# The DMAs of two output blocks, issued behind the next stage's first subtraction on GpSimd

## The chip, the cores and the metric

The kernel runs on one core of one Trainium2 chip. The metric is the device time of one launch in microseconds (us), the median of several runs. Beside it stands the profile of one execution. Its names for the engines are PE (TensorE, matmul), PEld (TensorE's weight load), DVE (VectorE), ACT (ScalarE), POOL (GpSimd) and SP (SyncE, which issues DMAs here); SPq and POOLq are the instruction queues of the last two. "L934" is line 934 of the kernel.

## The reference

Eight images of 512 channels, 32 x 32 pixels, float32. Each is group-normalized, goes through a C2f block with two attention bottlenecks, and is added to the input:

```python
x = x + _L0_conv_ref(_gn(x), ...)          # out = x + block(group_norm(x))

t = cbs(x, cv1_w, cv1_bn, 0)               # 1x1 conv 512 -> 512, batch norm, SiLU
ys = [t[:, :C], t[:, C:]]                  # C = 256
for i in range(N):                         # N = 2 bottlenecks
    yi = ys[-1]
    z = cbs(yi, m_cv1_w[i], m_cv1_bn[i], 1)                  # 3x3 conv 256 -> 256
    z = bot_attention(z, m_qkv_w[i], m_rw[i], m_rh[i])       # 4 heads of 64 over 1024 positions
    z = silu(bn_eval(conv2d(z, m_cv2_w[i], 0), m_cv2_bn[i])) # 1x1 conv
    ys.append(yi + z)
return cbs(concatenate(ys, axis=1), cv2_w, cv2_bn, 0)        # cv2: 1x1 conv 1024 -> 512
```

## The kernel before

**Pairs of images.** A loop `for p in range(NP)` treats the images in four pairs: the first image `ia` (a) and the second `ib` (b). In each pair, for bottleneck n = 0 and then n = 1, one 3x3 convolution (`conv3x3`) serves both images, and then the attention runs for image a and for image b. Work of other stages is put between the attention's steps: the group norm of the next pair, its cv1, and the final cv2. The convolution of n = 0 is called in this text the first one of the pair, that of n = 1 the second one.

**cv2 by blocks.** cv2 is one matrix product per image, 512 x 1024 times 1024 x 1024. `strassen` computes it as a 2 x 2 block product with seven block products. The result has four blocks, which `finish(i, ...)` puts out: i = 0 is C11, 1 is C12, 2 is C22, 3 is C21. `finish` works on two channel parts (`at` = 0, 1): ScalarE applies the SiLU into a tile `c_out`; a DMA from GpSimd's queue adds the input `x` from DRAM to that tile (`accum_op=ALU.add`, L1500); a second one stores the tile to `out` (L1501). The store must wait until the accumulating DMA has landed. That wait stands in GpSimd's own instruction queue, so everything queued behind it on GpSimd waits too.

For the second image of the pairs p = 0, 1, 2, `strassen` gets an argument `l2`: three of its seven products are then computed by quarter blocks (`by_quarters3`). In this variant `finish` gets a tile name (`room`) for two blocks: C12 with `l2.spare[0]`, the tile `p1`, and C21 with `l2.spare[1]`, the tile `p2`. C11 and C22 use a ring of four smaller tiles, `t`, and have no `room`. The last pair (p = 3) doesn't use `strassen` but other functions, with `finish` functions of their own. Image a of p = 0, 1, 2 goes through `strassen` without `l2`.

**Where the end of a pair meets the next one.** `part3` returns the last step, `lambda: finish(3, u3, l2.spare[1])`, which the loop keeps as `last_out`. The next pair hands it to its first convolution as `after`; it runs there behind the first PSUM copy on ScalarE. So C21 of one pair is put out while the next pair's first convolution is under way; C12 is put out just before it.

**The convolution and the projections behind it.** `conv3x3` runs over two output channel halves (`oc`) and three row groups (`i`), with products on PE, a PSUM copy on ScalarE (L680), and combinations on VectorE. The SiLUs of channel half 0 come when that half is done. In the second half, at `oc = 1, i = 1`, `conv3x3` calls `first_sum(summed, nc.gpsimd)`, which makes `t_z`, the difference of the two halves of the positions of channel half 0 of `z` (L934). The queries, keys and values are then computed by `project_strassen`, also a 2 x 2 block product. Its first products read `z`, the next ones read `t_z`:

```python
to_qk(ps_a, w["11"], b11)
if early:
    early()
to_qk(ps_b, w["s1"], t1)
```

(`t1` is `t_z`.) `project_strassen` also loads the position terms, `r_in` (L982), which VectorE adds at L986. The attention's first products are `l_ps` (L1080). In pair 0 the first convolution is another variant: it calls no `first_sum`.

**What sets the order.** Each engine runs its instructions in the order of its queue. A scheduler makes that order from the order in the program text; `tc.issue_after(ins)` adds that the instructions in its block come behind `ins` on the engine of `ins`. Around the change, GpSimd's queue holds the DMAs of `finish`, small memsets, the subtraction L934, and later the power and product of the group norm (L780, L837). SP's queue holds the loads: weights (`u`, `sq`, `sw`), the next images (`x`), `r_in`.

Of the kernel before, what the change touches and what calls it, by code (L numbers as in the profile page):

```python
# [48 lines left out]
ALU = mybir.AluOpType  # L49
# [13 lines left out]
def kernel(  # L63
# [16 lines left out]
    nc = tc.nc  # L80
# [8 lines left out]
    HALF = 512  # L89
# [107 lines left out]
    for tag in "qk":  # L197
        t = act.tile([P, NX // 2, HW], F32, tag=tag, name="x_second")
# [163 lines left out]
    def take_blocks(kind, n, which, names):  # L362
# [9 lines left out]
        out=gmat, in_=gmat, compare_op=ALU.is_ge, fill=0.0, base=0,  # L372
# [3 lines left out]
        out=gmat, in_=gmat, compare_op=ALU.is_ge, fill=0.0, base=GROUP - 1,  # L376
# [9 lines left out]
    spare = const.tile([P, 1], F32, name="spare")  # L386
# [111 lines left out]
    def by_slot(ap):  # L498
        a = ap.rearrange("p (h w) -> p h w", w=F) if len(ap.shape) == 2 else ap
        return a.rearrange("p h (j s) -> p h j s", j=4)  # L500

    def from_planes(ap):

        a = ap.rearrange("p (h w) -> p h w", w=F) if len(ap.shape) == 2 else ap
        return bass.AP(tensor=a.tensor, offset=a[:, :, 3:].offset, ap=[a.ap[0], a.ap[1], [-1, 4], [4, NT]])
# [7 lines left out]
    def stages(act, small, ps_big, ps_av, n_pt):  # L513

        def silu(dst, src, k):

            silued[0] = nc.scalar.activation(  # L517
                dst, src, AF.Silu, scale=sh[:, k : k + 1], bias=bh[:, k : k + 1]
            )
            return silued[0]  # L520
# [111 lines left out]
        def conv3x3(n, vs, u_of, z, groups=G, summed=None, after=None, between={}, silus=None):  # L632
# [10 lines left out]
            for oc in range(NM):  # L643
                dst = z[:, oc].rearrange("p g x -> p (g x)").rearrange("p (t r w) -> p r t w", r=4, w=F)
                for i in range(NI):
# [57 lines left out]
                    for (at, size), m in zip(parts, m_parts):  # L703
# [28 lines left out]
                        if i == 1:  # L732
                            if oc == NM - 1 and summed is not None:
                                t = first_sum(summed, nc.gpsimd)
# [154 lines left out]
        def project_direct(n, z, w, early=None, middle=None):  # L889
# [38 lines left out]
                qk(c)  # L928
            return q, kr, vT, lambda: None

        def first_sum(z, engine=nc.vector):

            t = act.tile([P, 2, HALF], F32, tag="pt", name="t_z", bufs=n_pt)
            engine.tensor_tensor(t[:, 0], z[:, 0, ts(1, HALF)], z[:, 0, ts(0, HALF)], ALU.subtract)  # L934
            return t

        def project_strassen(n, z, w, t, early=None, middle=None, table=False, silus=()):
# [517 lines left out]
        def strassen(b, ws, top, tags, tile_of, l2=None):  # L1455
# [34 lines left out]
            def rows_of(dram, i, at):  # L1490
                o, half = blocks[i]
                return dram[b, ts(2 * o + at, P), ts(half, HALF)]

            def finish(i, src, room=None):
                o, half = blocks[i]
                both = act.tile([P, 2, HALF], F32, tag=room, name="c_out") if room else None
                for at in range(2):
                    t = both[:, at] if room else act.tile([P, HALF], F32, tag="t", name="c_out", bufs=4)
                    silu(from_planes(t), by_slot(src[:, at, :]), bn_cv2 + 2 * o + at)
                    nc.gpsimd.dma_start(t, rows_of(x, i, at), accum_op=ALU.add)  # L1500
                    nc.gpsimd.dma_start(rows_of(out, i, at), t)  # L1501

            def part3(bottom, after=None):
                t1 = kept["t1"]
# [19 lines left out]
                for part in range(2):  # L1524
                    product(ps1, w12, bottom[0], [part], onto=True)
                    product(ps5, s4, bottom[1], [part], onto=True)
                finish(0, ps1)

                def new(name, t):
# [5 lines left out]
                c12 = tile_of("o1")  # L1535
                tt(c12, ps5, m1, ALU.add)
                finish(1, c12)
                tt(m1, new("s3", t3), m1, ALU.add)
                tt(m5, m5, m1, ALU.add)
                finish(2, m5)  # L1540
                tt(m1, m1, new("22", t4), ALU.subtract)
                return lambda: finish(3, m1)
# [404 lines left out]
    ps_big = fast.enter_context(tc.tile_pool(name="ps_big", bufs=3, space=PSUM))  # L1947
    ps_av = fast.enter_context(tc.tile_pool(name="ps_av", bufs=1, space=PSUM))
    s = stages(act, small, ps_big, ps_av, 6)

    def held(tag):
# [256 lines left out]
    for (i, cp), u in first_units.items():  # L2208
        fed["u", 0, 0, i, cp] = u

    last_out = None
    for p in range(NP):
        ia, ib = G * p, G * p + 1
        more = p + 1 < NP
# [3 lines left out]
        def u_of(n):  # L2218
            return lambda oc, i: [take(("u", n, oc, i, cp)) for cp in range(3)]

        def new_z():
            return act.tile([P, NM, G, HW], F32, tag="z", name="z")
# [50 lines left out]
        def direct_keys(which):  # L2273
# [6 lines left out]
        z = new_z()  # L2280
        silus = []
        t = s.conv3x3(
            0, vs, u_of(0), z, summed=None if direct else z[:, :, 0], after=last_out,
            between=in_first if direct else {}, silus=None if direct else silus,
        )
        xs = norm = None
        if more:
            if direct:
# [86 lines left out]
        if more and not direct:  # L2375
# [11 lines left out]
            with tc.issue_after(last.ins):  # L2387
                t = s.first_sum(z[:, :, 1])
# [7 lines left out]
        else:  # L2396
            if not direct:
                t = s.first_sum(z[:, :, 1])
# [139 lines left out]
        z = new_z()  # L2538
        t = s.conv3x3(1, vs, u_of(1), z, summed=z[:, :, 0], silus=silus)
# [80 lines left out]
        if not more:  # L2620
# [23 lines left out]
            l2 = SimpleNamespace(of=l_of, room=x_room)  # L2644
# [90 lines left out]
        def room_b(name):  # L2735
# [5 lines left out]

        b1, b1_more, b2, b3 = s.strassen(
            ib, w_of, top, {"m1": ("p3", 1), "m5": ("p4", 1)}, tile_of,
            SimpleNamespace(of=l_of, room=room_b, spare=("p1", "p2"))
        )
        b1()
        b1_more()
# [14 lines left out]
        last_out = b3(bottom)  # L2762
# [19 lines left out]
    with tc.If(held_all < P):  # L2782
        with ExitStack() as gs:
# [4 lines left out]
            make_identity(nc, ident)  # L2788
            g_av = gs.enter_context(tc.tile_pool(name="g_av", bufs=2, space=PSUM))
            g = stages(g_act, g_small, g_big, g_av, 3)  # L2790
            with tc.For_i(0, B, 1) as b:
                xts = [load_x(g_act, b, c, NX) for c in range(NX)]
# [6 lines left out]
                for n in range(N):  # L2799
# [5 lines left out]
                    z = g_act.tile([P, NM, 1, HW], F32, tag="z", name="z")  # L2805
# [69 lines left out]
```

## Time and profile before

| | us |
|---|---|
| median of three runs | 2239.03 (2238.82 to 2239.42) |
| the profiled execution | 2240.72 |
| its span, from the first to the last instruction | 2239.2 |
| DVE busy in the span | 1803.2 |
| ACT busy | 1093.4 |
| POOL busy | 223.3 |

The mean granted clock of TensorE is 0.993 of full speed. A group of instructions in the profile is one line, engine, operation and tile, with its count, its busy time, the mean of one in ns, the idle time of the engine just ahead of it, and what ended that idle time ("<-"). A timeline row has start, duration, engine, line, operation, output tile <- input tiles, shape and count; in brackets stands the idle time before it with its releaser. Matmuls are pipelined and their ends are modelled: distances between starts are safer than durations.

### The profile page before, as it was taken

What the parts mean: (1) busy time and instruction counts of PE and PEld (TensorE: products, weight loads), DVE (VectorE), ACT (ScalarE), POOL (GpSimd) and SP (SyncE); (2) the same over time, 40 slices, a digit from 0 to 9 for tenths busy, and PEclk for the clock granted to TensorE, in tenths of its full rate; (3) what the DMA queues carried; (4) which work ended last, traced back from release to release, by engine and by line L of the source; (5) the groups of instructions that cost most, each with busy time, mean ns of one, the idle gap of its engine ahead of it and who ended that gap; (6) DMA issues with size and microseconds to landing.
All of it is one profiled execution on the core that took longest, in us unless ns stands there. A gap on an engine that the chain in (4) does not pass through costs nothing.

```text
span 2239.2 us, 40840 instructions
## 1 busy us (share of the span) xinstructions
PE 2189.4 (98%) x16486; PEld 1112.7 (50%) x16486; DVE 1803.2 (81%) x2935; ACT 1093.4 (49%) x1320; POOL 223.3 (10%) x409
## 2 busy tenths in 40 slices
PE   7999999999989999999998999999999899999998
PEld 3653438343574444734457443564346734373445
DVE  8988879878887688977887768997787777897676
ACT  7455553654225666456323676455622365436543
POOL 4322210000220000000022000000002100000001
PEclk9999999999999999999999999999999999999999
DMA  8954447312591324512259141542126711251224
GB/s 269 314 163 141 160 148 257 100 48 71 155 310 48 115 84 135 194 59 67 69 138 306 33 153 47 179 140 77 58 67 180 274 39 40 95 192 39 76 58 114
DMA packets 135528, 291.93 MB, mean 130 GB/s; under 512 B 33732, under 2 KB 61376, under 8 KB 134308
## 3 DMA queue, kind: packets, MB, share of 16 engines
q1 hardware_dynamic: 102708, 201.01, 27.2%
q0 software_dynamic: 32624, 88.23, 13.3%
q8 instruction: 132, 2.16, 0.4%
q14 instruction: 64, 0.52, 0.1%
HBM read 219.58 MB, written 69.60 MB: 129 GB/s over the span
## 4 chain that ended last, share of the span: by engine, by line
PE 76%; DVE 8%; issue 7%; DMA 6%; POOL 1%; ACT 1%; SPq 0%; POOLq 0%; DVEq 0%; ACTq 0%
PE av_ps L1117 19%; PE l_ps L1080 18%; PE p_ps L956 7%; PE c_ps L675 6%; PE x_ps L1767 4%; PE m_ps L1334 4%; DMA c_out<-in_x_dram 4%; PE ps L545 4%; PE p_ps L962 3%; PE c L1354 3%; PE c_q L1402 2%; PE c_new L1354 2%; PE s_ps L1135 1%; DMA taps<-in_m_cv_w_dram 1%; PE c_new L1386 1%
## 5 line engine op out<-in xcount | busy, mean ns | idle before, releaser
L1084 ACT ACTIVATE pt<-l_ps 128x1024 f32<-128x1024 f32 x512 | 495.6, 1023 | 328.2 <-PE l_ps L1080 252.3
L1080 PE MATMUL l_ps<-q,kr 64*64 64x512 f32 x4096 | 485.5, 590 | 0.9 <-ACT pt L1084 0.9
L1117 PE MATMUL av_ps<-pt,vT 64*64 64x512 f32 x4096 | 484.7, 590 | 1.3 <-DVE z L1125 1.1
L1101 DVE TENSOR_TENSOR acc<-acc,pt 128x1024 f32<-128x1024 f32 x362 | 442.5, 1222 | 36.9 <-ACT pt L1084 9.8
L1117 PEld LDWEIGHTS av_ps<-pt,vT 64*64 64x64 f32 x4096 | 156.1, 133 | 280.6 <-issue 234.3
L1080 PEld LDWEIGHTS l_ps<-q,kr 64*64 64x64 f32 x4096 | 157.5, 133 | 270.3 <-issue 246.6
L675 PE MATMUL c_ps<-v_in,u 128*64 128x128 f32 x4320 | 238.5, 273 | 0.0
L675 PEld LDWEIGHTS c_ps<-v_in,u 128*64 128x64 f32 x4320 | 235.8, 137 | 4.9 <-issue 4.7
L956 PE MATMUL p_ps<-t_z,sq 128*128 128x512 f32 x224 | 111.6, 622 | 19.1 <-POOL t_z L934 19.1
L1125 DVE TENSOR_TENSOR z<-av_ps,z 128x512 f32<-128x512 f32 x64 | 43.9, 686 | 98.4 <-ACT z L1124 98.2
L1334 PE MATMUL m_ps<-z,m_sb 128*128 128x512 f32 x256 | 114.2, 593 | 0.1
L680 ACT COPY c_m<-c_ps 128x512 f32<-128x512 f32 x48 | 28.1, 585 | 152.4 <-PE c_ps L675 138.8
L517 ACT ACTIVATE t<-m_ps,bh,sh 128x512 f32<-128x512 f32 x64 | 46.3, 773 | 95.3 <-PE m_ps L1334 94.1
L1098 DVE TENSOR_TENSOR acc<-pt 128x1024 f32<-128x1024 f32 x64 | 78.0, 1219 | 14.2 <-PE s_ps L1135 8.7
L956 PE MATMUL p_ps<-z,sq 128*128 128x512 f32 x168 | 81.1, 603 | 0.7 <-ACT z L517 0.7
L1334 PEld LDWEIGHTS m_ps<-z,m_sb 128*128 128x128 f32 x256 | 47.7, 190 | 57.1 <-issue 51.4
L956 PEld LDWEIGHTS p_ps<-t_z,sq 128*128 128x128 f32 x224 | 40.7, 198 | 58.3 <-issue 34.7
L1193 DVE TENSOR_TENSOR z<-z,rs 128x512 f32<-128x512 f32 x64 | 42.3, 685 | 31.6 <-DMA rs<-r_dram 31.4
L517 ACT ACTIVATE z<-z,bh,sh 128x512 f32<-128x512 f32 x64 | 48.7, 809 | 25.2 <-DVE z L737 25.1
L962 PEld LDWEIGHTS p_ps<-sq,z 128*128 128x128 f32 x336 | 46.2, 201 | 23.8 <-issue 14.8
L1767 PE MATMUL x_ps<-t_x,sw 128*128 128x512 f32 x128 | 55.9, 592 | 0.0
L517 ACT ACTIVATE c_out<-c,bh,sh 128x512 f32<-128x512 f32 x12 | 14.0, 1277 | 85.7 <-PE c L1386 61.7
(408 smaller groups left out, 3301.7 us busy)
## 6 DMA issues: line engine op xcount, KB each, us to landing
u<-u SPq DMA_DIRECT2D x135, 512.0 KB
y_in<-y SPq DMA_DIRECT2D x32, 512.0 KB
rs<-r_dram SPq DMA_DIRECT2D x126, 128.0 KB
sq<-sq SPq DMA_DIRECT2D x42, 384.0 KB
x<-in_x_dram SPq DMA_DIRECT2D x28, 512.0 KB
r_in<-r SPq DMA_DIRECT2D x28, 512.0 KB
c_out<-in_x_dram POOLq DMA_DIRECT2D x56, 256.0 KB, 6.8
out_dram<-c_out POOLq DMA_DIRECT2D x56, 256.0 KB, 3.7
```

The source lines that it names most:

```text
L517: silued[0] = nc.scalar.activation(dst, src, AF.Silu, scale=sh[:, k : k + 1], bias=bh[:, k : k + 1])
L545: last_product[0] = nc.tensor.matmul(ps[:, half, :], w_of(k), rhs_of(k, half), start=(k == begin), stop=(k == end))
L675: conv_product[0] = nc.tensor.matmul(to[o], us[cp][:, k, row, c, o], rhs, start=(k == 0), stop=(k == NM - 1),)
L956: nc.tensor.matmul(ps[:, o, :], w[:, o, :], rhs, start=not onto, stop=True, skip_group_check=onto)
L962: nc.tensor.matmul(v[:, ts(j, P)], rhs[:, ts(j, P)], w[:, 2, :], start=j == 0 and not onto, stop=True, skip_group_check=True,)
L1080: nc.tensor.matmul(ps[kh * HD : (kh + 1) * HD, hd, :], kr[r, c, o : o + HD], q[r, c, ts(half, HALF)], start=True, stop=True,)
L1084: last_exp[0] = exp = nc.scalar.activation(pt, ps, AF.Exp, scale=SCALE)
L1101: ins = nc.vector.tensor_tensor(accs[g], accs[g], pt[i], ALU.add)
L1117: nc.tensor.matmul(avs[g][hd * HD : (hd + 1) * HD, kh, :], vT[r, j, o : o + HD], pt[i][r, hd, :], start=(j == 0), stop=(j == NJ - 1),)
L1334: nc.tensor.matmul(pss[half][:, oc, :], m2_sb[:, n, k, ts(oc, P)], ao[:, k, ts(half, HALF)], start=(k == 0), stop=(k == NM - 1),)
L1354: nc.tensor.matmul(ps[:, o, :], w[:, k, ts(o, P)], rhs[part][:, c], start=(k == 0 and not onto), stop=(k == KB - 1), skip_group_check=onto,)
L1767: nc.tensor.matmul(ps[:, o, :], w[:, c, ts(o, P)], rhs[c], start=(c == 0 and not onto), stop=(c == 1), skip_group_check=onto,)
```

## The change

`first_sum` keeps its instruction in `summing[0]`. In `finish`, the two DMAs of a channel part become a function `put_out`; where the block has a `room` (C12 and C21 of the second image), it isn't called but appended to the list `l2.late`. The next pair calls the functions in that list directly behind its first convolution's call, under `issue_after` with the kept subtraction. The SiLUs stay where they were, and so do the DMAs of C11 and C22.

```diff
+        summing = [None]
+
         def first_sum(z, engine=nc.vector):
 
             t = act.tile([P, 2, HALF], F32, tag="pt", name="t_z", bufs=n_pt)
-            engine.tensor_tensor(t[:, 0], z[:, 0, ts(1, HALF)], z[:, 0, ts(0, HALF)], ALU.subtract)
+            summing[0] = engine.tensor_tensor(t[:, 0], z[:, 0, ts(1, HALF)], z[:, 0, ts(0, HALF)], ALU.subtract)
             return t
...
                     silu(from_planes(t), by_slot(src[:, at, :]), bn_cv2 + 2 * o + at)
-                    nc.gpsimd.dma_start(t, rows_of(x, i, at), accum_op=ALU.add)
-                    nc.gpsimd.dma_start(rows_of(out, i, at), t)
+
+                    def put_out(t=t, at=at):
+                        nc.gpsimd.dma_start(t, rows_of(x, i, at), accum_op=ALU.add)
+                        nc.gpsimd.dma_start(rows_of(out, i, at), t)
+
+                    if room:
+                        l2.late.append(put_out)
+                    else:
+                        put_out()
...
-    last_out = None
+    last_out, late_outs = None, []
...
             0, vs, u_of(0), z, summed=None if direct else z[:, :, 0], after=last_out,
             between=in_first if direct else {}, silus=None if direct else silus,
         )
+        if late_outs:
+            with tc.issue_after(s.summing[0].ins):
+                while late_outs:
+                    late_outs.pop(0)()
...
-            SimpleNamespace(of=l_of, room=room_b, spare=("p1", "p2"))
+            SimpleNamespace(of=l_of, room=room_b, spare=("p1", "p2"), late=late_outs)
```

The list is filled in the pairs 0, 1 and 2 and emptied in the pairs 1, 2 and 3: each time four functions, eight DMAs.

## The prediction

> **What bounds the kernel now.** I read the page first (busy time, chain, costliest groups), then the chain of work between 625 and 700 us, then the timelines of GpSimd, ScalarE, VectorE and TensorE there. From the page:
>
> ```profile
> PE 2189.4 (98%) x16486; PEld 1112.7 (50%) x16486; DVE 1803.2 (81%) x2935; ACT 1093.4 (49%) x1320; POOL 223.3 (10%) x409
> ...
> L956 PE MATMUL p_ps<-t_z,sq 128*128 128x512 f32 x224 | 111.6, 622 | 19.1 <-POOL t_z L934 19.1
> ```
>
> TensorE (PE) is busy 98% of the span, so a change pays only where PE stands still or runs slowly. Of its idle time 19.1 us stands in one group: products on `t_z`, the tile that `first_sum` (line 934) writes on GpSimd. The GpSimd timeline shows why `t_z` is late:
>
> ```profile
> 646.52 1.82 POOL L1500 DMA_DIRECT2D c_out<-in_x_dram  x2
> 655.56 0.58 POOL L1501 DMA_DIRECT2D out_dram<-c_out  x1 [7.22 <-DMA c_out<-in_x_dram]
> ...
> 658.48 1.82 POOL L1500 DMA_DIRECT2D c_out<-in_x_dram  x2
> ...
> 670.50 0.57 POOL L1501 DMA_DIRECT2D out_dram<-c_out  x1 [2.29 <-DVE c_e L716]
> 671.08 1.27 POOL L934 TENSOR_TENSOR t_z<-z 128x512 f32<-128x512 f32 x1
> ```
>
> These are the blocks C12 and C21: two accumulating DMAs, two stores that wait for them to land, and the same again. GpSimd keeps its order, so the subtraction, last in the queue, starts at 671.08. Its input was long ready:
>
> ```profile
> 653.91 2.93 ACT L517 ACTIVATE z<-z,bh,sh 128x512 f32<-128x512 f32 x4 [1.79 <-DVE z L737]
> ```
>
> Those four SiLUs write the channel half that the subtraction reads; it needs the first two, done after about half of 2.93 us, near 655.4. What PE does meanwhile:
>
> ```profile
> 663.61 1.98 PE L956 MATMUL p_ps<-z,sq 128*128 128x512 f32 x4
> 672.41 3.78 PE L956 MATMUL p_ps<-t_z,sq 128*128 128x512 f32 x4 [6.82 <-POOL t_z L934]
> ...
> 677.60 1.06 PE L962 MATMUL p_ps<-sq,t_z 128*128 128x128 f32 x8
> ...
> 691.64 3.66 PE L1080 MATMUL l_ps<-q,kr 64*64 64x512 f32 x32
> ```
>
> The convolution ends at 663.61, four products on `z` follow, PE stands 6.82 us, and the first products afterwards take double.
>
> The kernel holds its own control: the second convolution of each pair ends in the same code (`conv3x3`, then `project_strassen`), with no stores ahead of the subtraction.
>
> ```profile
> 912.38 2.93 ACT L517 ACTIVATE z<-z,bh,sh 128x512 f32<-128x512 f32 x4 [3.16 <-DVE z L737]
> ...
> 913.98 1.27 POOL L934 TENSOR_TENSOR t_z<-z 128x512 f32<-128x512 f32 x1 [24.11 <-ACT z L517]
> ...
> 920.78 1.98 PE L956 MATMUL p_ps<-z,sq 128*128 128x512 f32 x4
> 922.60 1.88 PE L956 MATMUL p_ps<-t_z,sq 128*128 128x512 f32 x4
> ...
> 925.21 1.06 PE L962 MATMUL p_ps<-sq,t_z 128*128 128x128 f32 x8
> 926.43 1.98 PE L956 MATMUL p_ps<-z,sq 128*128 128x512 f32 x4 [0.17 <-ACT z L517]
> ...
> 939.96 3.66 PE L1080 MATMUL l_ps<-q,kr 64*64 64x512 f32 x32
> ```
>
> Here the subtraction starts 1.60 us after the SiLUs, and PE goes through at full pace. The table by stage, three first convolutions and then two of the second ones, each from the first `p_ps` product to attention:
>
> ```profile
> 663.60:691.70 28.10, 21.29 (x90) 0.88 0.52 171
> 1213.40:1240.90 27.50, 21.61 (x90) 0.88 0.55 179
> 1763.00:1790.70 27.70, 21.34 (x90) 0.88 0.56 184
> 920.70:940.00 19.30, 19.11 (x92) 1.00 0.48 156
> 1470.20:1489.50 19.30, 19.10 (x91) 1.00 0.49 158
> ```
>
> The columns are the window, its length, PE's busy time (instructions), granted clock, DMA share and GB/s. The same work takes 27.5 to 28.1 us with an 0.88 clock in one place and 19.3 us with a full clock in the other.
>
> **The change part by part.** *The move.* In each of the three pairs p = 1, 2, 3, eight GpSimd instructions (four accumulating DMAs, four stores) go from ahead of the subtraction to behind it. SiLUs, SP's DMAs and TensorE's order stay. The subtraction loses 671.08 − (653.91 + 1.60) = 15.6 us of queueing and would end near 656.8; PE wants it at 663.61 + 1.82 = 665.4 (1.82 is the step from 920.78 to 922.60). That leaves 8.6 us of cover, so the whole wait goes.
>
> *What it is worth.* I take the control's duration for all three places: 939.96 − 920.78 = 19.18 us. The places themselves, by their first and last rows:
>
> ```profile
> 1213.40 1.98 PE L956 MATMUL p_ps<-z,sq 128*128 128x512 f32 x4
> ...
> 1240.83 1.52 PE L1080 MATMUL l_ps<-q,kr 64*64 64x512 f32 x12
> ...
> 1763.03 1.98 PE L956 MATMUL p_ps<-z,sq 128*128 128x512 f32 x4
> ...
> 1790.66 1.93 PE L1080 MATMUL l_ps<-q,kr 64*64 64x512 f32 x13
> ```
>
> 691.64 − 663.61 = 28.03, 27.43 and 27.63: together 83.09, less 3 x 19.18 = 57.54, gives **25.5 us**. It splits into the 19.1 us of idleness and 6.4 us beside it. In the first place the products from 672.41 to 677.60 take 5.19 us, and the same ones in the control, from 922.60 to 925.21, 2.61: 2.6 us go to the slow clock, and some 0.5 of them the control loses in waits of its own (0.17 <-ACT z).
>
> *What is late next.* In the control, the next bounds are ScalarE's SiLU of the other channel half and VectorE's tail of the convolution. VectorE stands as follows relative to PE:
>
> ```profile
> 655.33 0.68 DVE L716 SCALAR_TENSOR_TENSOR c_e<-c_ps,c_t 128x512 f32<-128x512 f32 x1
> ...
> 913.79 0.68 DVE L716 SCALAR_TENSOR_TENSOR c_e<-c_ps,c_t 128x512 f32<-128x512 f32 x1
> 914.39 1.15 DVE L725 SCALAR_TENSOR_TENSOR c_r<-c_t 128x256 f32<-128x256 f32 x1
> 915.46 0.41 DVE L723 SCALAR_TENSOR_TENSOR c_r<-c_t,c_e 128x256 f32<-128x256 f32 x1
> ...
> 670.67 1.97 DVE L736 SCALAR_TENSOR_TENSOR z<-c_r,c_k 128x256 f32<-128x256 f32 x1
> ```
>
> It starts L716 8.28 us ahead of the first `p_ps` product (663.61 − 655.33), in the control 6.99 (920.78 − 913.79): it is 1.29 us better placed, so the control's waits shrink if anything. At best they go: the 0.19 us in which PE isn't busy in the control's window (19.30 − 19.11) and 0.10 for a group that restarts (1.98 at 926.43, 1.88 at 922.60), 0.9 us over three places: 26.4.
>
> *The collision with VectorE.* While the subtraction runs, a VectorE instruction is held: 1.97 us at 670.67, where a 128x256 one takes 0.41 (915.46). Moved, the subtraction hits VectorE inside its unbroken run; in the control that makes one instruction 1.15 instead of 0.41, 0.74 us, and this is already in the 19.18. The ends are nothing and 1.56 us each place, 4.7 in all, if the hold is as long as at 670.67 and comes out whole at PE; I take the control's, because its phase is the same (0.18 us after L716 begins, here 655.51 − 655.33).
>
> The Trainium skill (SBUF — State Buffer, SBUF: two separate sides) calls the port that these two engines share an exclusive lock, held for a whole instruction; that speaks against moving the subtraction into VectorE's busiest stretch. By it the hold could be the full 1.27 us, an estimate of 1.6 us more over three places than the control's; the trace shows a longer hold, 1.97 − 0.41 = 1.56 us, and the rows decide.
>
> *The moved DMAs.* Issues take 0.57 to 0.91 us each beside VectorE instructions of usual length (0.68 for 128x512 at 655.33), so issuing costs the other engines nothing visible. Behind them on GpSimd stands:
>
> ```profile
> 730.69 1.04 POOL L780 TENSOR_TENSOR gr<-gr,mhalf 128x4 f32<-128x4 f32 x1 [58.34 <-DVE gr L779]
> ...
> 1900.14 1.22 POOL L2368 DMA_DIRECT2D v<-v_new  x2 [128.82 <-DVE v_new L622]
> ```
>
> Two rounds of accumulate and store took 24.6 us (646.52 to 671.08). Begun at 656.8 they end near 681, and the next GpSimd instruction, some 9 us earlier than now, comes at 722: 41 us of cover, more in the last pair (1900). The tiles `p1` and `p2`, which now stay occupied until then, are next written by ScalarE behind the attention that follows (cv1's SiLUs, in the last pair the copies of m1 and m5). The transfers leave a stretch where the DMA engines are full and reach one where they have room:
>
> ```profile
> 658.40:671.00 12.60, 7.19 (x102) 5.71 (x98) 12.53 (x47) 1.60 (x2) 2.98 (x5) 0.99 1.05 368
> 671.00:691.70 20.70, 19.29 (x84) 12.33 (x86) 9.75 (x14) 9.07 (x14) 1.34 (x2) 0.84 0.33 111
> ```
>
> (the last two columns are again DMA share and GB/s). The first load that could suffer is `r_in`, which VectorE adds for attention:
>
> ```profile
> 653.67 0.84 SPq L982 DMA_DIRECT2D r_in<-r  x2
> ...
> 682.39 0.68 DVE L986 TENSOR_TENSOR kr<-p_ps,r_in 128x512 f32<-128x512 f32 x1
> ...
> 932.35 0.68 DVE L986 TENSOR_TENSOR kr<-p_ps,r_in 128x512 f32<-128x512 f32 x1
> ```
>
> It is issued 3 us before the moved DMAs and needed near 663.61 + 11.6 = 675 (932.35 − 920.78 in the control). I cost it at nothing; without that cover I bound it by what an accumulating DMA takes now to its store, 9 to 10 us (646.52 to 655.56), at one place.
>
> **The sum.** 2239.2 − 25.5 = 2213.7 us of span. The profiled execution took 2240.72 with 2239.2 of span; the median of the timed runs is 2239.03, so I take the saving from the median: 2213.5.
>
> **The rivals.** (1) *A new wait takes a part*: the hold on VectorE, or a SiLU behind it, delays the buffers or the inputs of PE. For it: VectorE is busy 12.53 of the 12.60 us from 658.40 to 671.00, so it makes up nothing. Against: it is further ahead than in the control. With 4.7 us lost the gain is 20.8: 2218.2. The exclusive lock of the Trainium skill (SBUF — State Buffer, named above) is a case of this rival.
> (2) *A load is late*: the moved transfers delay `r_in` or later loads. Two places at the bound of 10 us leave 5.5: 2233.5; one leaves 2223.5. Against: the DMA share of 0.33 there.
> (3) *The change doesn't do what it says*: the subtraction remains behind some DMA, since those of C11 and C22 precede it too. Against: they are issued by 646.52, 9 us ahead of its input. If the order stayed, 2239.0.
> (4) *Slower*: GpSimd is held by the moved stores when group norm's power (L780) is due; ScalarE then scales the next image late and the products of cv1 wait. It begins when two rounds last over 65 us instead of 24.6, and outweighs the gain where it costs over 12.8 us in each of the two pairs that have a group norm there, rounds of 78 us; at 85 us it would give 2239.0 + 2 x 20 − 25.5 = 2253.5. Against: transfers there have more room than now.
>
> **How the numbers follow.** The forecast has 0.82 (2212.6 to 2215.5), rival 1 0.10, rival 2 0.04, rival 3 0.02, rival 4 0.02. For 8 in 10 with the ends of the unknown costs, 26.4 and 20.8 of gain (2212.6 and 2218.2), and half a microsecond for the spread of the runs (2238.82 to 2239.42), the range is 2212.0 to 2218.5. A change under 0.2% (4.5 us) can't be told from none here. Faster takes the forecast, rival 1 and most of rival 2: 0.95; the same 0.03; slower 0.02.
>
> **What would show it.** Right: in the three places `t_z` starts some 1.6 us after the SiLUs, products on `t_z` lose their 19.1 us of idle time, the granted clock in the windows is 1.00, the windows shrink to 19.0 to 19.2 us, and everything else shifts. Wrong: a new releaser before `p_ps` or `l_ps` (VectorE `c_r`, DMA `r_in`), a subtraction that still follows a store, a longer wait at L780, or a convolution that became longer.

## The result, and the profile after

In one comparison of four runs each, the changed kernel took 2211.61 us (median; 2211.1 to 2212.26) and the kernel before 2238.93 us (2238.74 to 2239.42). The ratio is 0.9878, with a 95% interval of 0.9861 to 0.9895: 27.3 us less, where 25.5 were forecast. The time lies 0.4 us below the lower end of the range (2212.0). Over all comparisons of this study, the kernel before had 26 runs with a median of 2238.88 us (2235.66 to 2241.11), the changed one 12 runs with a median of 2212.03 us (2210.01 to 2213.35): 26.85 us less. The profiled execution of the changed kernel took 2212.26 us with a span of 2210.8.

The first two lines are from the page of the changed kernel, its busy times and its group of products on `t_z` (count, then busy us and mean ns, then the idle time ahead of them):

```profile
PE 2181.7 (99%) x16486; PEld 1109.3 (50%) x16486; DVE 1801.0 (81%) x2935; ACT 1094.1 (49%) x1320; POOL 222.9 (10%) x409
...
L958 PE MATMUL p_ps<-t_z,sq 128*128 128x512 f32 x224 | 105.9, 595 | 0.0
```

The 19.1 us of idle time ahead of that group are 0.0, and nothing stands in their place. The group's own 224 products take 105.9 us where they took 111.6: the clock no longer drops. The GpSimd timeline of the changed kernel at the first of the three places shows the new order:

```profile
644.72 0.57 POOL L1505 DMA_DIRECT2D out_dram<-c_out  x1 [3.38 <-DMA c_out<-in_x_dram]
654.63 1.28 POOL L936 TENSOR_TENSOR t_z<-z 128x512 f32<-128x512 f32 x1 [9.35 <-ACT z L517]
655.87 3.54 POOL L1504 DMA_DIRECT2D c_out<-in_x_dram  x4
663.40 0.57 POOL L1505 DMA_DIRECT2D out_dram<-c_out  x1 [3.99 <-DMA c_out<-in_x_dram]
...
671.31 0.54 POOL L1505 DMA_DIRECT2D out_dram<-c_out  x1 [2.24 <-DMA c_out<-in_x_dram]
720.53 1.04 POOL L780 TENSOR_TENSOR gr<-gr,mhalf 128x4 f32<-128x4 f32 x1 [48.69 <-DVE gr L779]
```

The subtraction now waits only for the SiLU. The four accumulating DMAs and four stores come behind it, and the next GpSimd instruction, L780, still waits 48.69 us for its input. TensorE's timeline at the same place, up to attention:

```profile
662.72 1.98 PE L958 MATMUL p_ps<-z,sq 128*128 128x512 f32 x4
664.54 1.88 PE L958 MATMUL p_ps<-t_z,sq 128*128 128x512 f32 x4
...
668.24 1.98 PE L958 MATMUL p_ps<-z,sq 128*128 128x512 f32 x4
...
670.95 1.88 PE L958 MATMUL p_ps<-z,sq 128*128 128x512 f32 x4
672.67 1.05 PE L964 MATMUL p_ps<-sq,z 128*128 128x128 f32 x8
673.56 1.88 PE L958 MATMUL p_ps<-t_z,sq 128*128 128x512 f32 x4
...
681.48 1.95 PE L1082 MATMUL l_ps<-q,kr 64*64 64x512 f32 x16
```

681.48 − 662.72 = 18.76 us, with no bracket in it. The table by stage of the changed kernel gives the three first convolutions and one second one (window, its length, busy time of PE, PEld, DVE, ACT and POOL, granted clock, DMA share, GB/s):

```profile
662.70:681.50 18.80, 18.77 (x89) 11.75 (x87) 16.19 (x51) 10.14 (x15) 2.23 (x4) 1.00 0.79 249
1203.00:1221.80 18.80, 18.77 (x88) 11.72 (x84) 16.19 (x51) 10.14 (x15) 2.22 (x4) 1.00 0.83 259
1743.30:1762.10 18.80, 18.77 (x88) 11.73 (x84) 16.19 (x52) 10.14 (x15) 2.23 (x4) 1.00 0.84 277
910.50:929.80 19.30, 19.11 (x88) 11.64 (x84) 17.52 (x54) 10.28 (x15) 0.00 (x0) 1.00 0.48 159
```

The first convolutions have become quicker than their control: 18.76 us, the control (910.62 to 929.80) still 19.18. The DMA share of 0.79 to 0.84 shows where the moved transfers went, into a stretch that had 0.52 to 0.56; PE doesn't feel it. By the windows the gain is 83.09 − 3 x 18.76 = **26.8 us**.

### The profile page after: what moved, and what is told of

It reads as the page before. It is cut to its first block, busy times and chain, and to the rows that moved or that the text cites. A ratio compares the mean times of both kernels' runs of the same rounds, so it can differ in the third digit from the quotient of the medians.

```text
span 2210.8 us, 40830 instructions
## 1 busy us (share of the span) xinstructions
PE 2181.7 (99%) x16486; PEld 1109.3 (50%) x16486; DVE 1801.0 (81%) x2935; ACT 1094.1 (49%) x1320; POOL 222.9 (10%) x409
## 3 DMA queue, kind: packets, MB, share of 16 engines
q1 hardware_dynamic: 102708, 201.01, 27.3%
## 4 chain that ended last, share of the span: by engine, by line
PE 91%; DVE 7%; ACT 1%; issue 1%; DMA 0%; POOL 0%; DVEq 0%; ACTq 0%
PE av_ps L1119 19%; PE l_ps L1082 18%; PE c_ps L675 10%; PE c L1356 7%; PE p_ps L958 7%; PE ps L545 5%; PE m_ps L1336 5%; PE x_ps L1776 4%; PE c_q L1404 4%; PE c_new L1356 3%; PE p_ps L964 3%; PE c L1388 2%; PE s_ps L1137 1%; PE c_new L1388 1%; DVE acc L1103 1%
## 5 line engine op out<-in xcount | busy, mean ns | idle before, releaser
L958 PE MATMUL p_ps<-t_z,sq 128*128 128x512 f32 x224 | 105.9, 595 | 0.0
L517 ACT ACTIVATE z<-z,bh,sh 128x512 f32<-128x512 f32 x64 | 48.7, 809 | 25.2 <-DVE z L737 25.0
```

The source lines that it names most:

```text
L517: silued[0] = nc.scalar.activation(dst, src, AF.Silu, scale=sh[:, k : k + 1], bias=bh[:, k : k + 1])
L958: nc.tensor.matmul(ps[:, o, :], w[:, o, :], rhs, start=not onto, stop=True, skip_group_check=onto)
```

## The experiments

Three theories stood at the start. **A**: the gain is that of the three windows alone, and they end at 18.76 us rather than 19.18 because VectorE stands further ahead there. **B**: the moved transfers help elsewhere too. **C**: what lies beyond 25.5 us is spread between executions. The table gives each run's time (median, and its ratio to the kernel before, timed on the same chip), the windows of the three first convolutions, and the rest: from the first `p_ps` product of pair 0's second convolution to the end of the span, so that a start that varies drops out. For before that is 2239.2 − 371.78 = 1867.4 us, for the changed kernel 2210.8 − 370.90 = 1839.9.

| run | us | ratio (95% interval) | windows, us | rest, us |
|---|---|---|---|---|
| again_after | 2212.85 | 0.9884 (0.9868 to 0.9901) | 18.76 each | 1840.9 |
| after_third | 2211.52 | 0.9877 (0.9860 to 0.9893) | 18.76 each | 1840.1 |
| no_late | 2212.58 | 0.9884 (0.9868 to 0.9901) | 18.76 each | 1840.0 |
| only_c12 | 2212.52 | 0.9885 (0.9869 to 0.9902) | 18.76 each | 1840.9 |
| only_c21 | 2213.67 | 0.9885 (0.9869 to 0.9902) | 18.76 each | 1840.7 |
| sum_vector | 2213.10 | 0.9885 (0.9868 to 0.9901) | 18.76 each | 1840.2 |
| lag_12 | 2213.01 | 0.9888 (0.9872 to 0.9905) | 19.10, 19.09, 19.10 | 1841.8 |
| lag_24 | 2217.21 | 0.9906 (0.9890 to 0.9923) | 18.76 each | 1844.9 |
| last_store | 2230.40 | 0.9963 (0.9949 to 0.9977) | 24.15, 23.53, 25.87 | 1857.6 |
| idle_25 | 2222.25 | 0.9926 (0.9909 to 0.9942) | 21.91, 22.88, 22.62 | 1852.6 |
| v_first | 2210.27 | 0.9872 (0.9856 to 0.9889) | 18.76 each | 1839.4 |

### The same kernel again: again_after, after_third

No edit: the changed kernel, timed in two further comparisons.

> The changed kernel once more, with five rounds, because its gain (27.3 us) is 1.8 us larger than forecast and a single interval is too wide for that. Theory A (the gain is the three windows and nothing else: 83.09 us before, 3 x 18.76 after, 26.8 us): 2238.9 - 26.8 = 2212.1, and windows of 18.7 to 18.8 us again. Theory B (the moved transfers also help elsewhere): a gain of 27.3 us or more again, 2211.6 or less. Theory C (the surplus is spread between executions): a gain nearer to 25.5 us, 2213.4.

> The changed kernel a third time, on the same chip and beside the same runs of the kernel before as v_first. Theory A: three windows of 18.76 us, and from the first window's start to the end of the span 1839.5 to 1841 us (1839.9 and 1840.9 in the two profiles so far, 1867.5 before), whatever the first 370 us take. Theory C has it that single executions differ in the windows too: a window outside 18.7 to 18.8.

The windows came out at 18.76 us six times more, and the rest between 1839.9 and 1840.9 us. The medians of the three comparisons, 2211.61, 2212.85 and 2211.52 us, lie on both sides of the range's end. The windows don't vary, and the rest by 1.0 us at most; most of the spread comes from the start: the first rows below are from TensorE's timeline of before, the second fence's from that of the changed kernel, at work that no edit touches.

```profile
74.90 3.71 PE L675 MATMUL c_ps<-v_in,u_new 128*64 128x128 f32 x64 [2.73 <-DVE v_in L629]
...
371.78 1.99 PE L956 MATMUL p_ps<-z,sq 128*128 128x512 f32 x4
```

```profile
74.03 3.71 PE L675 MATMUL c_ps<-v_in,u_new 128*64 128x128 f32 x64 [1.00 <-DVE v_in L629]
...
370.90 1.98 PE L958 MATMUL p_ps<-z,sq 128*128 128x512 f32 x4
```

In this pair, 0.9 us were there by 74 us. Over all profiled executions, with no edit ahead of it, the row near 371 starts between 368.85 and 371.81: 3 us of spread before the change has any part in it. Theory C is left with some tenths of a microsecond, the 27.3 us of the first comparison against the 26.8 of the windows.

### VectorE's lead: lag_12, lag_24

Both add instructions to VectorE in the first convolutions of pairs 1 to 3, at the second row group of channel half 1; each repeats the first of the two lines ahead of it and writes the same values. lag_12, shown here, has two of 0.68 us, which take away nearly all of VectorE's lead of 1.29 us over the control: its sum `c_k` of that row group (L730, in lag_12 L732) begins 0.17 us ahead of the first `p_ps` product, where it is 1.36 us in the changed kernel and 0.07 in the control. lag_24 has 4 in place of the 2.

```diff
-            turn, t = 0, None
+            turn, t, lag = 0, None, after is not None
...
                         tt(m[:, :, 0::2], slots(inner_ps, 0)[..., qs], m24[..., qs], ALU.add)
                         read = tt(m[:, :, 1::2], slots(inner_ps, 0)[..., qs], m24[..., qs], ALU.subtract)
+                        for _ in range(2 if lag and oc == 1 and i == 1 else 0):
+                            tt(m[:, :, 0::2], slots(inner_ps, 0)[..., qs], m24[..., qs], ALU.add)
```

> The changed kernel, with two VectorE instructions of the first convolution (L701, channel half 1, row group 1) done twice more in pairs 1, 2 and 3; they write the same values again. They put VectorE about 1.2 us later, to where it stands in the second convolutions. Theory A (the windows are 18.76 and not 19.18 us because VectorE stands 1.29 us earlier there): windows of 19.1 to 19.2 us, 0.4 us more each, 1.2 us in all over again_after. Theories B and C: windows stay at 18.76 and the time stays within 0.3 us of again_after.

> As lag_12, with four such instructions in place of two, some 2.4 us of VectorE work. Theory A: once VectorE sets the end, each further us on it appears in the window, so windows of 19.9 to 20.4 us, 1.2 to 1.6 us more each than in again_after, 3.6 to 4.9 us in all. Theories B and C: no difference to lag_12.

TensorE's timeline of lag_12, to be held against the changed kernel's above:

```profile
661.73 1.98 PE L960 MATMUL p_ps<-z,sq 128*128 128x512 f32 x4
...
667.29 1.98 PE L960 MATMUL p_ps<-z,sq 128*128 128x512 f32 x4
...
670.00 1.88 PE L960 MATMUL p_ps<-z,sq 128*128 128x512 f32 x4
671.90 1.16 PE L966 MATMUL p_ps<-sq,z 128*128 128x128 f32 x8
672.90 1.88 PE L960 MATMUL p_ps<-t_z,sq 128*128 128x512 f32 x4
```

From the third group on `z` in this fence to the next one on `t_z` it takes 672.90 − 670.00 = 2.90 us, where the changed kernel takes 673.56 − 670.95 = 2.61. That is the control's own figure, as TensorE's timeline of the changed kernel shows for the second convolution:

```profile
910.62 1.98 PE L958 MATMUL p_ps<-z,sq 128*128 128x512 f32 x4
...
916.28 1.98 PE L958 MATMUL p_ps<-z,sq 128*128 128x512 f32 x4 [0.17 <-ACT z L517]
...
918.99 1.88 PE L958 MATMUL p_ps<-z,sq 128*128 128x512 f32 x4
920.89 1.16 PE L964 MATMUL p_ps<-sq,z 128*128 128x128 f32 x8
921.88 1.88 PE L958 MATMUL p_ps<-t_z,sq 128*128 128x512 f32 x4
```

921.88 − 918.99 = 2.89. So the lead makes most of what the first convolutions are shorter by than the control, and theory A holds in the main. The control's extra 0.42 us has two parts: 0.13 at the SiLU (916.28 − 910.62 = 5.66, against 668.24 − 662.72 = 5.52) and 0.28 here. The window of lag_12 closes 0.34 of the 0.42 us (19.10): the 0.28 in full, but only 0.04 of the 0.13 at the SiLU (667.29 − 661.73 = 5.56), and no run shows where the other 0.09 come from. A further 0.20 us a place is lost ahead of the window: the convolution, from its first product to the first `p_ps` product, takes 31.79 us where it takes 31.59 in before and in the changed kernel. Its whole time can't be told from that of again_after, measured beside it.

For lag_24 the window was expected to grow and did not; the loss came ahead of it, as TensorE's timeline of lag_24 shows:

```profile
662.33 1.97 PE L675 MATMUL c_ps<-v_in,u 128*64 128x128 f32 x32 [1.42 <-ACT c_m L680]
664.23 1.98 PE L960 MATMUL p_ps<-z,sq 128*128 128x512 f32 x4
```

The view of waits has `4.3, 3, 1.4` us for this wait (in all, times, longest). With VectorE later still, TensorE waits inside the convolution (33.24 us in place of 31.59), its last products come later, and VectorE has its lead back by the time the window begins. The total, 4.4 us over again_after, was in the expected bounds, the place was not. That the wait comes from PSUM tiles that VectorE frees late is my reading; no run isolates it.

### The moved DMAs: no_late, only_c12, only_c21

no_late (first diff) leaves out the 24 moved DMAs, so the blocks C12 and C21 of three images are not written. The other two move one block and leave the other where it was; the second diff is only_c12, and only_c21 has `spare[1]`.

```diff
-                    if room:
-                        l2.late.append(put_out)
-                    else:
+                    if not room:
                         put_out()
```

```diff
-                    if room:
+                    if room and room == l2.spare[0]:
                         l2.late.append(put_out)
```

> The changed kernel without the moved DMAs: the accumulating DMAs and the stores of C12 and C21 of the second image of pairs 0, 1 and 2 are left out altogether (24 DMAs), so these blocks of the output aren't written. It prices what the moved DMAs cost where they are now. Theory A: they cost nothing, the time is that of again_after within 0.5 us. The rival that moved transfers delay loads of the next stage: faster than again_after by over 1 us. Theory B in the form that their absence from the convolution helps: no further gain.

> The other half: only the DMAs of C12 go behind the subtraction, those of C21 stay ahead of it. By the prediction's cover one round ahead of the subtraction is hidden whichever it is: the whole gain, the time of the changed kernel within 1 us. Rival (C21, put out last, is what counts): the subtraction waits for a round that ends as late as before, and most of the gain is gone, 2230 or more.

> Half of the change: only the DMAs of C21 go behind the subtraction, those of C12 stay ahead of it. By the prediction's cover: the first round of accumulate and store ended at 658.5 us before, so the subtraction would end near 660, 5 us before TensorE wants it (665.4): the whole gain, the time of the changed kernel within 1 us. Rival (each of the two rounds costs half of the wait): half of the gain, 2225.

The table by stage of no_late, first place:

```profile
661.50:680.30 18.80, 18.77 (x87) 11.73 (x86) 16.18 (x51) 10.14 (x15) 0.00 (x0) 1.00 0.40 127
```

With half the DMA share (0.40 instead of 0.79) the window and the rest are the same, and the time is 0.3 us from that of again_after beside it. So the moved transfers cost nothing and help nothing that these runs can show: theory B falls. The GpSimd timeline of only_c21, where C12's round stays ahead of the subtraction:

```profile
646.97 1.82 POOL L1504 DMA_DIRECT2D c_out<-in_x_dram  x2
656.28 0.58 POOL L1505 DMA_DIRECT2D out_dram<-c_out  x1 [7.50 <-DMA c_out<-in_x_dram]
658.64 0.57 POOL L1505 DMA_DIRECT2D out_dram<-c_out  x1 [1.78 <-DMA c_out<-in_x_dram]
659.23 1.29 POOL L936 TENSOR_TENSOR t_z<-z 128x512 f32<-128x512 f32 x1
```

One round of accumulate and store, 12.3 us, holds the subtraction back to 659.23, and it still ends at 660.5, 5.5 us before PE wants it (the window starts at 664.2, and 1.82 us later comes the first product on `t_z`). So moving either block alone brings the whole gain, by the windows: the 8.6 us of cover hide one round, not two. The time of only_c21 is 1.6 us above the 2212.03 of the changed kernel's 12 runs, where at most 1 us was expected; these runs themselves cover 3.3 us.

### The dose: last_store

Here only the last store of C21 is put behind the subtraction; the accumulating DMAs and the other three stores stay ahead of it.

```diff
                     def put_out(t=t, at=at):
-                        nc.gpsimd.dma_start(t, rows_of(x, i, at), accum_op=ALU.add)
                         nc.gpsimd.dma_start(rows_of(out, i, at), t)
-                    if room:
+                    nc.gpsimd.dma_start(t, rows_of(x, i, at), accum_op=ALU.add)
+                    if i == 3 and at == 1 and room:
                         l2.late.append(put_out)
```

> Of the eight DMAs at each place only the very last one, the store of the second channel part of C21, goes behind the subtraction. The subtraction can then start when the store before it is issued (668.2, 1217.4 and 1767.8 us in the trace of before in place of 671.08, 1219.95 and 1770.04): TensorE's idle time shrinks from 6.8, 5.9 and 6.4 us to 3.9, 3.3 and 4.1. If the slow clock comes with an idle time of this length too: a gain of 7.7 us, 2231.2, the first products on t_z still taking double. If the clock stays up: about 7.8 us more, 2223.4.

GpSimd's and then TensorE's timeline of last_store:

```profile
666.86 0.58 POOL L1504 DMA_DIRECT2D out_dram<-c_out  x1 [7.31 <-DMA c_out<-in_x_dram]
667.45 1.28 POOL L936 TENSOR_TENSOR t_z<-z 128x512 f32<-128x512 f32 x1
```

```profile
663.17 1.98 PE L958 MATMUL p_ps<-z,sq 128*128 128x512 f32 x4
668.79 3.48 PE L958 MATMUL p_ps<-t_z,sq 128*128 128x512 f32 x4 [3.63 <-POOL t_z L936]
...
1214.09 2.67 PE L958 MATMUL p_ps<-t_z,sq 128*128 128x512 f32 x4 [3.14 <-POOL t_z L936]
...
1761.64 3.54 PE L958 MATMUL p_ps<-t_z,sq 128*128 128x512 f32 x4 [5.29 <-POOL t_z L936]
```

One store less in front shortens the idle time from 19.1 to 3.63 + 3.14 + 5.29 = 12.1 us: by 3.2, 2.8 and 1.1 us. The first two are near what was expected, the wait of this store and its issue (2.29 + 0.57 us in the first place); the third missed, because there the round itself ran 0.8 us later against the convolution and the subtraction took 1.69 us instead of 1.27. The windows are still 17.3 us above 3 x 18.76, so 5.2 us of it stand beside the idle time, and the view of windows gives a granted clock of 0.93 in all three: the slow clock again. The gain, 8.6 us, is near the 7.7 expected for that case.

### The queue alone: sum_vector

The kernel before, with the first convolutions' subtraction on VectorE and all DMAs where they were.

```diff
-            turn, t = 0, None
+            turn, t, first = 0, None, after is not None
...
-                                t = first_sum(summed, nc.gpsimd)
+                                t = first_sum(summed, nc.vector if first else nc.gpsimd)
```

> The kernel before, with its DMAs where they were, but with the first convolutions' subtraction on VectorE in place of GpSimd, in pairs 1, 2 and 3. If GpSimd's queue is the whole cause, the wait goes here as well: the time of the changed kernel within 1 us, windows of 18.7 to 18.9 us (0.6 us of VectorE work added, 0.74 us of hold removed). Rival (the DMAs themselves, by transfers or by their place, are what costs): the windows shorten by less, and the time stays over 2215.

The VectorE timeline of sum_vector shows the subtraction in its run:

```profile
656.53 0.68 DVE L934 TENSOR_TENSOR t_z<-z 128x512 f32<-128x512 f32 x1
```

It costs VectorE 0.60 us there and saves it the hold that it has in the changed kernel, 0.74 us (below). With no DMA moved, the windows are the same 18.76 us: the subtraction's place in GpSimd's queue was the whole cause. The time, 2213.10 us, is 1.1 us above the changed kernel's 2212.03, just over the 1 us expected and within the spread of its runs.

### An idle time made on purpose: idle_25

It is meant to give TensorE a known idle time with nothing else late, to see when the clock drops: the first convolutions' subtraction is made late, behind a small GpSimd instruction that waits for ScalarE's copy `u`, and the moved DMAs come behind that, issued behind the call of `project_strassen`.

```diff
-            turn, t = 0, None
+            turn, t, first = 0, None, after is not None
...
-                            if oc == NM - 1 and summed is not None:
+                            if oc == NM - 1 and summed is not None and not first:
                                 t = first_sum(summed, nc.gpsimd)
...
-            t1, t2 = t[:, 0], t[:, 1]
+            late = t is None
...
+            if late:
+                nc.scalar.copy(u, ps_a)
+                tick = small.tile([P, 1], F32, tag="gr", name="tick")
+                ticked = nc.gpsimd.tensor_tensor(tick, u[:, 0, 0:1], u[:, 0, 0:1], ALU.subtract)
+                with tc.issue_after(ticked.ins):
+                    t = first_sum(z, nc.gpsimd)
+            t1, t2 = t[:, 0], t[:, 1]
             to_qk(ps_b, w["s1"], t1)
             to_v(ps_v[:, 0], w["11"], b11)
-            nc.scalar.copy(u, ps_a)
+            if not late:
+                nc.scalar.copy(u, ps_a)
...
```

> The changed kernel, with the first convolutions' subtraction (pairs 1, 2 and 3) begun only after ScalarE's copy of the first p_ps products, which GpSimd reads with one small instruction first. The subtraction then ends some 2.5 us after TensorE wants it. It asks from which idle time on the slow clock comes. If an idle time of 2.5 us suffices: windows of 18.76 + 2.5 + 1.5 = 22.8 us, the four products on t_z taking over 3 us, 12 us more in all than after_third. If the clock stays up: windows of about 21.3 us, 7.5 us more in all, the four products taking 1.9 us.

The table by stage of idle_25, the three places:

```profile
662.80:684.80 22.00, 19.09 (x90) 11.87 (x92) 16.62 (x47) 10.04 (x15) 7.41 (x10) 1.00 0.76 202
1206.20:1229.20 23.00, 20.79 (x92) 12.86 (x88) 16.65 (x48) 10.04 (x15) 7.43 (x10) 0.93 0.71 193
1752.10:1774.80 22.70, 20.61 (x92) 12.73 (x88) 16.60 (x48) 10.13 (x15) 7.46 (x10) 0.92 0.82 228
```

TensorE's timeline of idle_25, the first and the second place:

```profile
667.68 1.98 PE L958 MATMUL p_ps<-t_z,sq 128*128 128x512 f32 x4 [1.99 <-POOL t_z L936]
...
1211.15 2.96 PE L958 MATMUL p_ps<-t_z,sq 128*128 128x512 f32 x4 [1.99 <-POOL t_z L936]
```

PE stands 1.99 us ahead of these products in each of the three places. One kept the full clock, two didn't, so the outcome that was expected, one or the other throughout, missed; the whole time is 10.7 us above after_third, between the two that were forecast (7.5 and 12). The scheduler also put eight products on `z` ahead of those on `t_z`, and even at full clock the first window is 21.91 − 18.76 − 1.99 = 1.16 us longer, as PE waits another 0.92 us there for a SiLU. So something else was late too: the run tells of the clock only and is no clean price of a late subtraction.

### A version beyond: v_first

The control loses 0.28 us where ScalarE's copy of `q` waits for VectorE's last read of a work tile (L727) that shares its buffer, with the copy of `vT` behind it, although that one could go. v_first swaps the two copies in `project_strassen`.

```diff
-            nc.scalar.copy(q0, ps_a[:, 0])
+            with tc.issue_after(nc.scalar.copy(v0, v_of(ps_v[:, 0])).ins):
+                nc.scalar.copy(q0, ps_a[:, 0])
             add_r(0, 0, ps_a[:, 1])
-            nc.scalar.copy(v0, v_of(ps_v[:, 0]))
```

> The changed kernel, with two ScalarE copies in project_strassen in the other order: the values' copy (v0) ahead of the queries' copy (q0), which in the second convolutions waits for VectorE's last read of the tile that q takes over. Theory A (VectorE's position makes the difference of 19.18 and 18.76 us; 0.29 of the 0.42 us by that copy's place in ScalarE's queue, 0.13 by the SiLU): the four second windows go from 19.18 to about 18.89 us, the three first ones stay at 18.76, 1.2 us less in all than after_third. If the wait lies elsewhere: windows as before, no difference.

ScalarE's timeline of the changed kernel in the second convolution shows the wait:

```profile
919.76 0.59 ACT L1012 COPY q<-p_ps 128x512 f32<-128x512 f32 x1 [1.52 <-DVE c_r L727]
920.25 0.59 ACT L1014 COPY vT<-p_ps 128x512 f32<-128x512 f32 x1
```

TensorE's timeline of v_first in the second convolution:

```profile
919.55 1.88 PE L958 MATMUL p_ps<-z,sq 128*128 128x512 f32 x4
921.27 0.94 PE L964 MATMUL p_ps<-sq,z 128*128 128x128 f32 x7
```

The products follow after 1.72 us as in the first convolutions, not after 1.90, and all four windows of the second convolutions are 18.90 instead of 19.19 us. The time was 2210.27 us (2209.46 to 2212.67), that of the changed kernel beside it 2211.52 (2210.01 to 2213.21): the 1.25 us agree with 4 x 0.29, but the runs overlap, so the windows carry this and not the time. Its median is the lowest here.

## Why the prediction was nearly right, and what missed

**The bound and the move: right.** The queue of GpSimd was the whole cause (sum_vector). The subtraction begins 1.60 us after the SiLUs, as forecast (654.63, the SiLUs at 653.03), and ends at 655.91, 8.63 us before PE wants it at 664.54; the forecast said 8.6. That cover carries a round of DMAs (only_c12, only_c21).

**The worth: mis-sized, and this is the step that failed.** "I take the control's duration for all three places: 19.18 us." It measured 18.76, so the term of 57.54 us is 56.28 and the gain 26.8 us, not 25.5. The prediction had the reason in hand, VectorE's 1.29 us of lead, and drew from it only that the waits "shrink if anything". lag_12 shows that this lead is worth 0.34 us of the 0.42 in the window; no run isolates the other 0.08.

**The best case was too small too.** It took the control's PE idle time, 0.19 us, and one restart of 0.10: 0.29 a place, 26.4 us. Distances between starts would have given 0.42: the control's eight products on `z` appear as 1.16 us where an undisturbed group has 1.05, so a part of the wait stands inside what the view counts as busy.

**The spread: too narrow.** The half microsecond came from three runs (2238.82 to 2239.42). The 26 runs of before cover 5.5 us, the 12 of the changed kernel 3.3. With a gain of 26.8 the forecast would be 2239.03 − 26.8 = 2212.2, at the edge of the range, and such a spread decides on which side a median falls.

**Beside the idle time: right.** The gain is 19.1 us of idle time and 26.8 − 19.1 = 7.7 beside it; the prediction's split had 6.4, and the difference is again the control's own 3 x 0.42 us. The first products after an idle time run at the slow clock in last_store too, and in no place of the changed kernel.

**The collision with VectorE: right.** The VectorE timeline of the changed kernel has the hold that was taken over from the control, 1.15 us instead of 0.41 or 0.42:

```profile
654.44 0.68 DVE L716 SCALAR_TENSOR_TENSOR c_e<-c_ps,c_t 128x512 f32<-128x512 f32 x1
655.04 1.15 DVE L725 SCALAR_TENSOR_TENSOR c_r<-c_t 128x256 f32<-128x256 f32 x1
656.12 0.41 DVE L723 SCALAR_TENSOR_TENSOR c_r<-c_t,c_e 128x256 f32<-128x256 f32 x1
...
673.01 0.68 DVE L988 TENSOR_TENSOR kr<-p_ps,r_in 128x512 f32<-128x512 f32 x1
```

The exclusive lock of the Trainium skill (SBUF — State Buffer, SBUF: two separate sides) was priced at a full hold of 1.27 us. L725 comes 0.41 us after the subtraction, so only 655.91 − 655.04 = 0.87 us of it were left, near the hold of 1.15 − 0.41 = 0.74: the trace agrees in kind. The price was nothing: the convolution takes 31.59 us in the changed kernel, with the hold in it, and in before, where the hold came later, and PE doesn't stand still in the window behind it. (sum_vector alone doesn't show this, since it trades the 0.74 us of hold for 0.60 us of VectorE's own work.)

**The moved DMAs at nothing: right** (no_late). The last store is issued at 671.31, 48.7 us before L780, not near 681 as worked out from two rounds.

**The rivals.** A new wait (1) and a late load (2) would show as idle time in the windows: PE is busy 18.77 of the 18.80 us in all three, and the addition of `r_in`, the last row above, begins 673.01 − 662.72 = 10.29 us into the window, in the control 11.57. The order unchanged (3) and the slower case at L780 (4) are excluded by the GpSimd timeline.

## What to carry to other kernels

In this kernel a store that waited for an accumulating DMA on GpSimd held every later instruction of that engine, here a ready subtraction for 15.6 us; what PE needs soon is to be put ahead of such rounds, or on another engine, and the room ahead of PE's need tells how many rounds may stay. A control within the same kernel gives the mechanism, but its time is to be corrected for how far each engine stands ahead, by distances between starts and not by idle time alone. The spread for a range comes from more than three runs.

## What the runs showed of the hardware

**The clock can drop after short idle times.** After 1.99 us of idle time the granted clock of the window was 1.00 in one place and 0.93 and 0.92 in two (idle_25). The drop is a step: taken by half microseconds, the view of windows has a granted clock of 0.50 from 1212.0 to 1215.4 us in the second place, 3.4 us, begun 0.9 us after PE had started again, and of 1.00 before and after. At the first place of the kernel before it lasts twice as long, from 670.7 to 677.5 us, the first 1.7 us of it while PE stood. Half a clock over 3.4 us of work costs 1.7 us. In last_store, 3.63, 3.14 and 5.29 us of idle time cost 24.15 − 18.76 − 3.63 = 1.76, 1.63 and 1.82 us beside themselves. In before, 6 to 7 us cost 7.7 us beside themselves over the three places, 2.6 each. The Trainium skill (TensorE: Matmul & The Clock Gate, HAM oscillation — how this bites in real kernels) gives as a rule to have no idle gaps over some 3.4 us; two of these three gaps of 1.99 us were already too long, and the measurement decides. Why the third kept its clock is open.

**Four accumulating DMAs at once took less time here than two and two.** Issued back to back from 655.87, they were followed by the last of their stores at 671.31 (0.54 us), 16.0 us in all; the two rounds of before took 24.6 us. How much of that is the issue in one block and how much the other load of the DMA engines is open.
